# Graph attention on one core: steps summed as A (E - 1) g moved and added, and the first pass's row loads moved into the second and third cycle

## The chip, the cores and the metric

The kernel runs on one core of a Trainium2 chip. The metric is the device time of one launch in microseconds (us); lower is better.

## The reference

Two layers work on x (4096 nodes, 512 features) and a 0/1 adjacency matrix A (4096 x 4096). The first layer is attention with eight heads of 64 features each; the second is a scaled attention inside 32 blocks of 128 nodes. The change touches only the first layer:

```
feats  = einsum('nf,hfo->hno', X, W)
s_self = einsum('hno,ho->hn', feats, a_self)
s_neigh = einsum('hno,ho->hn', feats, a_neigh)
dense  = leaky_relu(s_self[:, :, None] + s_neigh[:, None, :], 0.2) * A
attn   = softmax(dense, axis=-1)
out    = relu(einsum('hij,hjo->hio', attn, feats) + b)      # then x = layernorm(x + out)
```

A pair that is no edge still has the weight exp(0) = 1. So the sum over the neighbours is the sum over all nodes plus, for the edges alone, the sum of (E - 1) feats, with E = exp(leaky_relu(...)).

## The kernel before

**Passes, chunks, steps and cycles.** The heads are worked in pairs: four passes (`r` = 0 to 3). A pass goes over four chunks (`c`) of 1024 output nodes, and a chunk over 32 steps (`j`) of 128 neighbour nodes. Steps are issued in cycles: eight steps to a cycle in passes 0 to 2 (`wide=8`: a chunk's cycles begin at j0 = 0, 8, 16, 24), four in pass 3. The "last cycle" of a chunk below is j0 = 24 in pass 0 and j0 = 28 in pass 3.

**A plain step.** VectorE makes, for each of the pair's two heads, a tile `q` of 128 x 1024 (line 1534): max(p_row, d_j) times the adjacency tile `at`. TensorE then does two things. At line 1558 it subtracts the plain features over the edges: two weight tiles `f_s` times `at`, in two halves, so four matmuls into `accf`. At line 1581 it adds `g_s` times `q` into `acc`. A mark of each `q` (ScalarE at line 1544, for one `q` in eight VectorE at line 1539) goes into `dens` (line 1597).

**A folded step**, summed as A (E - 1) g. VectorE makes `q` with two operations a head: max(p_row, d_j) times a further row `U_row` (line 1522), then minus a column `c_all`, times `at` (line 1525). The matmuls of line 1558 are left out, the matmuls of line 1581 add to `accf` and not to `acc`, and ScalarE makes both marks (line 1529). `folded(j)` says which steps are folded; it does so in passes 0 and 3 alone (`FOLDED`).

**Order within a cycle on TensorE.** Its order is the program's: the line 1558 matmuls of all the cycle's steps; transposes of adjacency for the next cycle (pass 0, line 617); in pass 3 pieces of the second layer (`PLAN`, `PLANS`); the line 1581 matmuls; after every eighth step those of line 1597; in pass 0 the sums `ae` and a second lot of transposes. The other engines' queues are filled by a planner, in the order in which it expects work to be ready; where two instructions are ready, the traces show the one that was written first going first. `in_order(True, ins)` keeps an instruction behind those written before it.

**End of a chunk.** `sums_to_rows` reads `accf` (line 1278: plus `S_col`, times `u_row`, into `ys`) and then `acc` (line 1286); `accf` and `acc` have one buffer each. Since `u_row` has one buffer too, the next chunk's is loaded after line 1278. Each of the two `p_row` has two buffers.

**Where the adjacency comes from.** In pass 0 POOL's queue loads blocks `a_b` (line 605, four bytes an element in memory, one on the chip, three buffers), TensorE transposes them, ScalarE casts them to `at` (line 628), and POOL's queue stores each to `at_d` (line 629). Later passes load `at` from `at_d` on SP's queue, which also carries `p_row` (line 1434), `u_row` (line 1440), `U_row` (line 1462), `f_s` (line 1496) and `g_s` (line 1501). In pass 0 `U_row` lies in the two buffers named `ck`.

**Buffers that the prediction uses.** The ring of `q` has 8 tiles in pass 0 and 6 in pass 3. The second layer's results in PSUM (`ps_m`) share three banks in pass 3, taken in turn.

**Second layer beside pass 3.** The pieces `a` and `b` in the plan work on two blocks of 512 nodes. In the last cycle of chunks 1 and 2 the plan says "aaba": two output products (line 1200), which VectorE reads at line 1202 into `y_f`; two value products (line 1186), read by VectorE at line 1194; the scores of the other block (line 1141), read at line 1150; two more output products.

Of the kernel before, what the change touches and what calls it, by code (L numbers as in the profile page):

```python
# [10 lines left out]
F32 = mybir.dt.float32  # L11
# [8 lines left out]
P = 128  # L20
# [378 lines left out]
def broadcast_rows(v, parts, n):  # L399

    return bass.AP(tensor=v.tensor, offset=v.offset, ap=[[0, parts], [1, n]])
# [3 lines left out]
def adjacency_streamed_path(  # L405
# [29 lines left out]
    nc = tc.nc  # L435
    N, F = x.shape
    H, _, FH = W.shape
    NT = N // P
    FC = F // P
    PR = H // 2  # L440
    FP = 2 * FH
# [3 lines left out]
    C = 1024  # L445
    CT = C // P
    NCH = N // C
# [14 lines left out]
    g_d = dram.tile([PR, NT // 4, P, 4 * FP], F32, name="g_d")  # L462
    f_d = dram.tile([PR, NT // 4, P, 4 * 2 * FP], F32, name="f_d")
    FOLDED = (0, PR - 1)
    FOLDS = {4: (1,), 5: (0, 1), 6: (0, 1, 2)}, {2: (1,), 4: (1,), 5: (0, 1), 6: (0, 1, 2)}
    HU = 2 * len(FOLDED)
    pu_d = dram.tile([2 * H + HU, N], F32, name="pu_d")
    at_d = dram.tile([NCH, NT, P, C], F32, name="at_d")
# [73 lines left out]
    rowp = ctx.enter_context(tc.tile_pool(name="rows_f", bufs=2))  # L542
    urowp = ctx.enter_context(tc.tile_pool(name="urows", bufs=1))
# [46 lines left out]
    def in_order(pinned, ins):  # L590

        if pinned:
            tc.keep_in_program_order(ins)
# [29 lines left out]
    def cast_steps(c, j, pt, steps=range(2)):  # L623

        both = pt.rearrange("p t n -> p (t n)").bitcast(FP8).rearrange("p (n k) -> p n k", k=2)
        for k in steps:
            at = ats[0, c, j + k] = ring("at", atp, 6).tile([P, C], F32R, name="at")
            ends_of_setup["ACT"] = nc.scalar.copy(at, both[:, :, k])  # L628
            nc.gpsimd.dma_start(at_d[c, j + k], at.bitcast(F32))  # L629
# [9 lines left out]
    with tc.tile_pool(name="setup1", bufs=1, side="right") as one, tc.tile_pool(  # L639
        name="setup_rows", bufs=1, side="right"  # L640
    ) as late, tc.tile_pool(name="setup2", bufs=2, side="right") as two, tc.tile_pool(
        name="xtp", bufs=4, side="right"
    ) as xtp, tc.tile_pool(name="staged1", bufs=1, side="right") as staged1, tc.tile_pool(
        name="staged2", bufs=2, side="right"
    ) as staged2, tc.tile_pool(
        name="ps_setup", bufs=3, space=PSUM
    ) as pss, tc.tile_pool(name="ps_feat", bufs=2, space=PSUM) as psf:
        NB = NT // 4
        xts, xTs, pu_js, rows = {}, {}, {}, {}
# [773 lines left out]

    steps = [(r, c, j) for r in range(PR) for c in range(NCH) for j in range(NT)]

    def main_pass(r, ae=None, wide=4):

        for c in range(NCH):
            p_row = []
            for h in range(2):  # L1430
                p_row.append(rowp.tile([P, C], F32, name=f"p_row{h}"))
                in_order(
                    r == 0 and c < 2,
                    nc.sync.dma_start(p_row[h], broadcast_rows(pu_d[2 * r + h, ts(c, C)], P, C)),
                )
            u_row = urowp.tile([P, C], F32, name="u_row")
            for h in range(2):
                in_order(
                    r == 0 and c < 2,
                    nc.sync.dma_start(  # L1440
                        u_row[h * FH : (h + 1) * FH, :],
                        broadcast_rows(pu_d[H + 2 * r + h, ts(c, C)], FH, C),
                    ),
                )
            U_row = []

            def folded(j):

                if r == PR - 1:
                    return r in FOLDED and c > 0 and j % 4 in FOLDS[c > 1].get(j // 4, ())  # L1450
                return r in FOLDED and j % 8 == 2 and (0 if c else 8) < j < NT - 8

            def rows_for_folded():

# [35 lines left out]
            for j0 in range(0, NT, wide):  # L1490
                at_step = steps.index((r, c, j0))
                cycle = range(j0, j0 + wide)
                f_s, g_s = {}, {}
                for k in range(j0 // 4, (j0 + wide) // 4):
                    f_s[k] = fsp.tile([P, 4, 2, FP], F32R, name="f_s")
                    ins = nc.sync.dma_start(
                        f_s[k].rearrange("p u s n -> p (u s n)").bitcast(F32), f_d[r, k]
                    )
                    in_order(r == 0 and c == 0 and j0 < 16, ins)
                    g_s[k] = gfp.tile([P, 4, 2, FH], F32, name="g_s")  # L1500
                    ins = nc.sync.dma_start(
                        g_s[k].rearrange("p u h o -> p (u h o)"), g_d[r, k]
                    )
                    in_order(r == 0 and c == 0 and j0 < 16, ins)
                if at_step == 0:
                    cast_steps(0, 6, last_pair)
                if any(map(folded, range(NT))) and j0 == (4 if r else 0):
                    rows_for_folded()
# [6 lines left out]
                for j in cycle:  # L1515
                    for h in range(2):
# [3 lines left out]
                        if folded(j):  # L1520
                            cn = c_all[r][:, j, h : h + 1]
                            nc.vector.scalar_tensor_tensor(
                                q, p_row[h], d_j, U_row[h], op0=OP.max, op1=OP.mult
                            )
                            nc.vector.scalar_tensor_tensor(  # L1525
                                q, q, cn, ats[r, c, j].bitcast(F32), op0=OP.subtract, op1=OP.mult
                            )
                            mark = marks[j, h] = sgp.tile([P, C], FP8, name="mark")
                            nc.scalar.activation(  # L1529
                                mark, q, AF.Sigmoid, bias=below_0, scale=2.0**80, saturate=False  # L1530
                            )
                            continue
# [5 lines left out]
                        if j % 4 == 3 and h == 1:  # L1538
                            nc.vector.tensor_scalar(  # L1539
                                mark, q, d_j, None, op0=OP.is_gt, saturate=False  # L1540
# [14 lines left out]
                for j in cycle:  # L1555
                    for w in range(0 if folded(j) else 2):
                        for s in range(2):
                            nc.tensor.matmul(  # L1558
                                accf[:, s, :],
                                f_s[j // 4][:, j % 4, w, :],  # L1560
                                ats[r, c, j][:, ts(s, HB)],
                                start=(j == 0 and w == 0),
                                stop=(j == NT - 1 and w == 1),
                            )
# [11 lines left out]
                for j in cycle:  # L1576
                    dst = accf if folded(j) else acc
                    for s in range(2):
                        for o in range(0, FP, 32):
                            h = o // FH  # L1580
# [47 lines left out]
    with tc.tile_pool(name="ps_ae", bufs=1, space=PSUM) as psx:  # L1628
        ae = psx.tile([P, HB], F32, name="ae")
        nc.vector.memset(ae, 0.0)  # L1630
        banks.append(psx)
        main_pass(0, ae, wide=8)
        banks.remove(psx)
    first_pass.close()
    banks.extend([ctx.enter_context(tc.tile_pool(name="ps_misc2", bufs=2, space=PSUM))] * 2)
    with tc.tile_pool(name="wl1", bufs=1, side="right") as wp:
        work.append(weights_of_layer_1(keep, wp))
        work.append(kind_of_graphs(wp))
        work.append(kind_of_scores(wp))
        main_pass(1, wide=8)  # L1640
        for gen in work:
            for _ in gen:
                pass
        work.clear()
    main_pass(2, wide=8)
    more.clear()
    wide_passes.close()
    with tc.tile_pool(name="lp", bufs=2) as lp, tc.tile_pool(
        name="lp1", bufs=1
# [7 lines left out]
@with_exitstack  # L1657
def tile_gat_then_graph_attention(ctx: ExitStack, tc: tile.TileContext, *args: bass.AP):
    nc = tc.nc
    keep = ctx.enter_context(tc.tile_pool(name="flag", bufs=1))  # L1660
    flag = keep.tile([1, 1], I32, name="flag")
    adjacency_streamed_path(tc, flag, *args)
    other = nc.values_load(flag[0:1, 0:1], min_val=0, max_val=1)
    with tc.If(other > 0):
        general_path(tc, *args)
# [42 lines left out]
```

## Time and profile before

| | before |
|---|---|
| three runs | 2040.04, 2040.63, 2043.24 us (median 2040.63) |
| the profiled execution | 2043.19 us |
| its span | 2041.3 us |
| TensorE matmul busy | 2005.9 us (98%) |
| VectorE busy | 1744.8 us (85%) |
| ScalarE busy | 1533.1 us (75%) |
| folded tiles of q (line 1525) | 62, for 31 steps |

The span is the profile's time from the first to the last instruction; the execution's own time has 1.9 us around it. Times in the trace count from the start of the span. A busy TensorE can hold short waits, since matmuls are pipelined and their ends are modelled; where it matters, the starts of neighbouring matmuls are compared. In a group's row the first number after the bar is busy time in us, the second the mean of one instruction in ns.

### The profile page before, as it was taken

What the parts mean: (1) busy time and instruction counts of PE and PEld (TensorE: products, weight loads), DVE (VectorE), ACT (ScalarE), POOL (GpSimd) and SP (SyncE); (2) the same over time, 40 slices, a digit from 0 to 9 for tenths busy, and PEclk for the clock granted to TensorE, in tenths of its full rate; (3) what the DMA queues carried; (4) which work ended last, traced back from release to release, by engine and by line L of the source; (5) the groups of instructions that cost most, each with busy time, mean ns of one, the idle gap of its engine ahead of it and who ended that gap; (6) DMA issues with size and microseconds to landing.
All of it is one profiled execution on the core that took longest, in us unless ns stands there. A gap on an engine that the chain in (4) does not pass through costs nothing.

```text
span 2041.3 us, 38200 instructions
## 1 busy us (share of the span) xinstructions
PE 2005.9 (98%) x14981; PEld 1030.0 (50%) x14981; DVE 1744.8 (85%) x2219; ACT 1533.1 (75%) x1872; POOL 231.0 (11%) x362
## 2 busy tenths in 40 slices
PE   8999999999999999999999999999999999999997
PEld 7885545444444444444444544444444444445443
DVE  5668898898999998798999989999997897889754
ACT  3348988788888889788899889999786566567420
POOL 1222222222200000000000000000020210211111
PEclk9999999999999999999999999999999999999999
DMA  6899999999999999788999999989975775775211
GB/s 206 240 320 280 283 286 288 285 280 282 316 377 342 346 359 342 261 311 292 318 321 338 313 328 338 335 277 368 323 277 186 249 255 173 232 273 176 73 55 44
DMA packets 209386, 558.70 MB, mean 274 GB/s; under 512 B 25052, under 2 KB 66012, under 8 KB 209196
## 3 DMA queue, kind: packets, MB, share of 16 engines
q1 hardware_dynamic: 144844, 433.65, 61.0%
q0 software_dynamic: 62272, 121.98, 23.3%
q8 instruction: 120, 1.97, 0.4%
q10 hardware_dynamic: 2080, 0.52, 0.1%
q14 instruction: 70, 0.57, 0.1%
HBM read 499.13 MB, written 107.28 MB: 297 GB/s over the span
## 4 chain that ended last, share of the span: by engine, by line
PE 85%; DMA 7%; DVE 5%; issue 1%; ACT 1%; SPq 0%; POOL 0%; POOLq 0%; DVEq 0%; ACTq 0%
PE acc L1581 35%; PE accf L1558 20%; PE ps_fe L818 5%; PE ps_m L1186 5%; PE ps_m L1114 5%; PE dens L1597 5%; DMA a_b<-in_adj_dram 4%; DVE q L1534 3%; PE accf L1581 2%; PE ps_m L1141 1%; PE ps_m L1200 1%; DMA hp_l<-hs_d 1%; PE ps_m L617 1%; DMA at_d<-at 1%; PE ps_m L1043 1%
## 5 line engine op out<-in xcount | busy, mean ns | idle before, releaser
L1534 DVE SCALAR_TENSOR_TENSOR q<-p_row,d_all,at 128x1024 f32<-128x1024 f32 x962 | 1168.1, 1279 | 106.0 <-PE acc L1581 78.8
L1544 ACT ACTIVATE mark<-q,nb_all 128x1024 fp8e4<-128x1024 f32 x834 | 926.8, 1144 | 174.7 <-DVE q L1534 160.1
L1581 PE MATMUL acc<-q,g_s 128*32 128x512 f32 x7696 | 853.7, 594 | 1.1 <-DVE q L1534 0.4
L1581 PEld LDWEIGHTS acc<-q,g_s 128*32 128x32 f32 x7696 | 250.2, 110 | 557.2 <-issue 496.3
L1558 PE MATMUL accf<-at,f_s 128*128 128x512 f32 x1924 | 469.3, 400 | 1.7 <-ACT at L628 1.6
L1558 PEld LDWEIGHTS accf<-at,f_s 128*128 128x128 f32 x1924 | 357.2, 189 | 107.3 <-issue 27.8
L1249 ACT ACTIVATE ck<-ck,neg_half_f 128x1024 f32<-128x1024 f32 x128 | 146.0, 1141 | 28.5 <-DMA ck<-in_adj_dram 28.4
L1250 ACT ACTIVATE ck<-ck,neg_quarter 128x1024 f32<-128x1024 f32 x128 | 146.3, 1143 | 1.8
L1597 PE MATMUL dens<-mark,e_b 128*6 128x512 fp8e4 x2048 | 125.3, 379 | 2.5 <-DVE mark L1539 2.5
L818 PE MATMUL ps_fe<-w_sb_f,xT_f 128*128 128x264 f32 (+1 forms) x512 | 121.6, 395 | 1.7 <-ACT xT_f L730 1.7
L628 ACT CAST at<-ps_m 128x1024 fp32r<-128x1024 fp8e4 x124 | 116.3, 1022 | 4.8 <-issue 2.0
L1186 PE MATMUL ps_m<-wvT,x1T 128*128 128x512 f32 x256 | 114.2, 594 | 0.0
L1114 PE MATMUL ps_m<-x1T,M_sb 128*128 128x512 f32 x256 | 113.1, 595 | 0.0
L818 PEld LDWEIGHTS ps_fe<-w_sb_f,xT_f 128*128 128x128 f32 x512 | 100.5, 200 | 16.2 <-ACT xT_f L730 2.3
L1372 POOL DMA_DIRECT2D hs_d<-hst x12 | 10.7, 896 | 828.1 <-DVE hst L1362 817.5
L1539 DVE TENSOR_SCALAR mark<-q,d_all 128x1024 fp8e4<-128x1024 f32 x128 | 96.2, 751 | 4.7
L629 POOL DMA_DIRECT2D at_d<-at x128 | 69.1, 540 | 272.5 <-ACT at L628 94.0
L1597 PEld LDWEIGHTS <-e_b 128*6 128x6 bf16 x2048 | 55.9, 86 | 80.1 <-issue 38.2
L1529 ACT ACTIVATE mark<-q,below 128x1024 fp8e4<-128x1024 f32 x62 | 69.6, 1153 | 24.5 <-DVE q L1525 24.2
L1114 PEld LDWEIGHTS ps_m<-x1T,M_sb 128*128 128x128 f32 x256 | 48.0, 190 | 58.9 <-issue 57.1
L1525 DVE SCALAR_TENSOR_TENSOR q<-q,c_all,at 128x1024 f32<-128x1024 f32 x62 | 77.3, 1273 | 0.0
L1186 PEld LDWEIGHTS ps_m<-wvT,x1T 128*128 128x128 f32 x256 | 47.7, 190 | 56.3 <-issue 55.1
(207 smaller groups left out, 1294.9 us busy)
## 6 DMA issues: line engine op xcount, KB each, us to landing
at<-at_d SPq DMA_DIRECT2D x384, 512.0 KB, 6.1
f_s<-f_d SPq DMA_DIRECT2D x128, 512.0 KB, 7.8
at_d<-at POOLq DMA_DIRECT2D x128, 512.0 KB, 19.1
ck<-in_adj_dram SPq DMA_DIRECT2D x128, 512.0 KB, 5.5
g_s<-g_d SPq DMA_DIRECT2D x128, 256.0 KB, 5.9
f_d<-fst POOLq DMA_DIRECT2D x16, 1024.0 KB, 7.5
a_b<-in_adj_dram POOLq DMA_DIRECT2D x32, 512.0 KB, 21.7
p_row<-pu_d SPq DMA_DIRECT2D x32, 512.0 KB, 6.7
```

The lines of the kernel that those rows point to most:

```text
L628: ends_of_setup["ACT"] = nc.scalar.copy(at, both[:, :, k])
L818: nc.tensor.matmul(pf[:, q, :, cols], tile_j(xTs[k][:, c].rearrange("p u n -> p (u n)"), u), w_sb[:, c, 4 * q : 4 * q + 4, cols], start=(c ...
L1114: nc.tensor.matmul(pz, L1["M"][:, f, ts(c, P)], x1T[:, f, :], start=(f == 0), stop=(f == FC - 1),)
L1186: nc.tensor.matmul(pv, x1T[:, f, ts(u, P)], L1["wvT"][:, f, :], start=(f == 0), stop=(f == FC - 1),)
L1249: tc.keep_in_program_order(nc.scalar.activation(ck, ck, AF.Square, bias=neg_half))
L1250: nc.scalar.activation(ck, ck, AF.Abs, bias=neg_quarter, accum_out=binp[:, k : k + 1])
L1534: ends_of_setup["Q"] = nc.vector.scalar_tensor_tensor(q, p_row[h], d_j, ats[r, c, j].bitcast(F32), op0=OP.max, op1=OP.mult)
L1539: nc.vector.tensor_scalar(mark, q, d_j, None, op0=OP.is_gt, saturate=False)
L1544: nc.scalar.activation(mark, q, AF.Sigmoid, bias=nb_all[:, j, hh : hh + 1], scale=BIG, saturate=False,)
L1558: nc.tensor.matmul(accf[:, s, :], f_s[j // 4][:, j % 4, w, :], ats[r, c, j][:, ts(s, HB)], start=(j == 0 and w == 0), stop=(j == NT - 1 an ...
L1581: nc.tensor.matmul(dst[o : o + 32, s, :], g_s[j // 4][:, j % 4, h, o % FH : o % FH + 32], qs[j, h][:, ts(s, HB)], start=(j == 0), stop=(j ...
L1597: nc.tensor.matmul(dens[lo : lo + 6, :], e_b[:, j, 2 * r + h, :], marks[j, h][:, ts(s, HB)], start=(j == 0), stop=(j == NT - 1),)
```

## The change

Which steps are folded: in pass 0 they were j = 10 and 18 in chunk 0 and j = 2, 10, 18 in chunks 1 to 3 (11 in all); now they are j = 8, 16, 24 in every chunk (12). In pass 3 they were six in chunk 1 and seven each in chunks 2 and 3 (20); now chunks 1 and 2 have j = 28 and 29 as well (24). Of a block of `f_s` that has folded steps, only the stretch from its first to its last plain step is loaded. In pass 0 `u_row` of chunks 1 to 3 is asked for in the chunk's second cycle, and both `p_row` of the next chunk in the third cycle, all kept in program order.

```diff
-    FOLDS = {4: (1,), 5: (0, 1), 6: (0, 1, 2)}, {2: (1,), 4: (1,), 5: (0, 1), 6: (0, 1, 2)}
+    FOLDS = {1: {4: (1,), 5: (0, 1), 6: (0, 1, 2), 7: (0, 1)}, 2: {2: (1,), 4: (1,), 5: (0, 1), 6: (0, 1, 2), 7: (0, 1)}, 3: {2: (1,), 4: (1,), 5: (0, 1), 6: (0, 1, 2)}}
...
+    p_rows = {}
+
+    def load_p_rows(r, c, pinned):
+
+        rows = []
+        for h in range(2):
+            rows.append(rowp.tile([P, C], F32, name=f"p_row{h}"))
+            ins = nc.sync.dma_start(rows[h], broadcast_rows(pu_d[2 * r + h, ts(c, C)], P, C))
+            in_order(pinned, ins)
+        return rows
+
+    def load_u_row(r, c, pinned):
+
+        u_row = urowp.tile([P, C], F32, name="u_row")
+        for h in range(2):
+            ins = nc.sync.dma_start(
+                u_row[h * FH : (h + 1) * FH, :],
+                broadcast_rows(pu_d[H + 2 * r + h, ts(c, C)], FH, C),
+            )
+            in_order(pinned, ins)
+        return u_row
...
         for c in range(NCH):
-            p_row = []
-            for h in range(2):
-                p_row.append(rowp.tile([P, C], F32, name=f"p_row{h}"))
-                in_order(
-                    r == 0 and c < 2,
-                    nc.sync.dma_start(p_row[h], broadcast_rows(pu_d[2 * r + h, ts(c, C)], P, C)),
-                )
-            u_row = urowp.tile([P, C], F32, name="u_row")
...
+            p_row = p_rows.pop((r, c), None) or load_p_rows(r, c, (r, c) == (0, 0))
+            if r or c == 0:
+                u_row = load_u_row(r, c, r == 0)
...
-                    return r in FOLDED and c > 0 and j % 4 in FOLDS[c > 1].get(j // 4, ())
-                return r in FOLDED and j % 8 == 2 and (0 if c else 8) < j < NT - 8
+                    return r in FOLDED and c > 0 and j % 4 in FOLDS[c].get(j // 4, ())
+                return r in FOLDED and j % 8 == 0 and j > 0
...
+                    live = [u for u in range(4) if not folded(4 * k + u)]
                     ins = nc.sync.dma_start(
-                        f_s[k].rearrange("p u s n -> p (u s n)").bitcast(F32), f_d[r, k]
+                        f_s[k][:, live[0] : live[-1] + 1].rearrange("p u s n -> p (u s n)").bitcast(F32),
+                        f_d[r, k, :, live[0] * 2 * FP : (live[-1] + 1) * 2 * FP],
                     )
...
+                if r == 0 and c and j0 == 8:
+                    u_row = load_u_row(r, c, True)
+                if r == 0 and c < NCH - 1 and j0 == 16:
+                    p_rows[r, c + 1] = load_p_rows(r, c + 1, True)
```

More of the change, by code (lines that the diff above doesn't have):

```diff
@@ L1424, in adjacency_streamed_path @@
     steps = [(r, c, j) for r in range(PR) for c in range(NCH) for j in range(NT)]
+    p_rows = {}
[15 more added lines that the diff above has]
+        return u_row
     def main_pass(r, ae=None, wide=4):
         for c in range(NCH):
-            p_row = []
-            for h in range(2):
-                p_row.append(rowp.tile([P, C], F32, name=f"p_row{h}"))
-                in_order(
-                    r == 0 and c < 2,
-                    nc.sync.dma_start(p_row[h], broadcast_rows(pu_d[2 * r + h, ts(c, C)], P, C)),
-                )
-            u_row = urowp.tile([P, C], F32, name="u_row")
[L1437 to L1444, printed above, removed]
+            p_row = p_rows.pop((r, c), None) or load_p_rows(r, c, (r, c) == (0, 0))
+            if r or c == 0:
+                u_row = load_u_row(r, c, r == 0)
             U_row = []
```

## The prediction

> **What bounds the kernel now.** I read the busy shares first, then the rows of the operations concerned, then pass 0 and pass 3 cycle by cycle, since an average over the span hides where a wait ends last. From the page:
>
> ```profile
> PE 2005.9 (98%) x14981; PEld 1030.0 (50%) x14981; DVE 1744.8 (85%) x2219; ACT 1533.1 (75%) x1872; POOL 231.0 (11%) x362
> L1525 DVE SCALAR_TENSOR_TENSOR q<-q,c_all,at 128x1024 f32<-128x1024 f32 x62 | 77.3, 1273 | 0.0
> L1558 PE MATMUL accf<-at,f_s 128*128 128x512 f32 x1924 | 469.3, 400 | 1.7 <-ACT at L628 1.6
> ```
>
> TensorE has only 35 us without a matmul in flight, so a matmul removed is time gained wherever VectorE keeps up. Line 1558 costs 469.3/1924 = 0.244 us each; a fold removes four, 0.98 us, and adds two VectorE operations of 77.3/62 = 1.25 us.
>
> Busy time by stretch, last cycle of pass 0's chunk 1 and first two of chunk 2 (columns: span, PE, PEld, DVE, ACT, POOL, granted clock, DMA share, GB/s):
>
> ```profile
> 343.00:369.00 26.00, 26.00 (x248) 13.33 (x246) 22.18 (x21) 23.15 (x23) 5.73 (x10) 1.00 1.10 303
> 369.00:401.00 32.00, 28.00 (x245) 12.49 (x243) 25.47 (x30) 24.75 (x26) 7.70 (x13) 0.95 1.12 258
> 401.00:427.00 26.00, 26.00 (x248) 13.07 (x246) 24.35 (x25) 22.83 (x23) 6.08 (x10) 1.00 1.12 283
> ```
>
> A chunk's first cycle takes 32 us where its neighbours take 26, and DMA is full throughout. The waits of TensorE in pass 0, its timeline and that of SP say why:
>
> ```profile
> PE ps_m L617 <- DMA a_b<-in_adj_dram: 6.2, 3, 3.6
> ...
> 379.89 1.07 PE L617 MATMUL ps_m<-ident_b,a_b 128*128 128x128 bf16 x16 [3.63 <-DMA a_b<-in_adj_dram]
> ...
> 352.38 1.09 SPq L1440 DMA_DIRECT2D u_row<-pu_d  x2
> ...
> 362.38 1.51 SPq L1434 DMA_DIRECT2D p_row<-pu_d  x2
> ...
> 352.91 26.93 DMA a_b<-in_adj_dram
> ```
>
> The three waits (0.41, 3.63 and 2.19 us) stand in the first cycles of chunks 1, 2 and 3. Each late block was asked for at a chunk's end, beside 0.5 MB of `u_row` and 1 MB of `p_row`, and took 26.5 to 28 us; the median is 21.7. After the 3.63 us TensorE ran slowly too: line 1581's weight loads stand 0.86 us apart for 3.4 us, against 0.43, another 1.7 us. Recoverable: 6.2 + 1.7 = 7.9 us.
>
> Pass 3, last cycle of chunk 1 (chunk 2's is alike), timelines of VectorE and TensorE:
>
> ```profile
> 1568.74 3.68 DVE L1534 SCALAR_TENSOR_TENSOR q<-p_row,d_all,at 128x1024 f32<-128x1024 f32 x3 [8.14 <-PE accf L1581]
> 1573.00 6.06 DVE L1534 SCALAR_TENSOR_TENSOR q<-p_row,d_all,at 128x1024 f32<-128x1024 f32 x5
> 1578.98 0.74 DVE L1202 SCALAR_TENSOR_TENSOR y_f<-ps_m,rd_f,x1b 128x512 f32<-128x512 f32 x1
> 1579.64 1.27 DVE L1278 SCALAR_TENSOR_TENSOR ys<-accf,S_col,u_row 128x1024 f32<-128x1024 f32 x1
> ...
> 1577.53 1.88 PE L1200 MATMUL ps_m<-v_t,a 128*128 128x512 f32 x4
> 1579.24 7.03 PE L1186 MATMUL ps_m<-wvT,x1T 128*128 128x512 f32 x16
> ...
> 1610.96 3.11 PE L1581 MATMUL acc<-q,g_s 128*32 128x512 f32 x16 [0.21 <-DVE q L1534]
> ```
>
> VectorE idles 8.14 us, but before these q tiles, since the ring of six is full; it then works without a gap until it reads the first output product at 1578.98. Half a chunk on, TensorE already waits for q.
>
> [...] after the 3.63 us gap 3.4 us at half speed, none after the 2.19 us one. [...] SP's rows beside POOL's `a_b`, DMA share 1.10. [...]
>
> **The change part by part.**
>
> *Pass 0, matmuls.* Three folds leave first cycles, four enter last ones, those of third cycles stay: 12 for 11, net -0.98 us.
>
> *Pass 0, VectorE in the last cycle.* It has 3.7 us idle around line 1278 (2.16 + 1.54 in chunk 1); the fold's second operations take 2.4 at the 1.2 us pitch. Line 1278 now needs the fold's g too, 1.75 us into the line 1581 phase. By then step 28's q is ready to start and was written first, so I take line 1278 to follow step 31's q: `accf` is then read about 5 us before the next chunk's first matmul. Zero. Were it put ahead, step 31's q would be 0.5 us late in each of four chunks: 0 to +2.
>
> *Pass 0, rows.* `u_row` (0.5 MB) moves from near 352 to 288 in chunk 1's example, `p_row` (1 MB) from 362 to 314, behind `g_s` on SP; neither buffer is then in use and both rows are wanted over 40 us later. `U_row` (1 MB, in `ck`) is released by step 24, not 18, so its load moves towards the border, from 318 to about 342. Near the late block 1.5 MB leave and 1 MB comes 10 us ahead of it; `f_s` is 128 KB smaller in three blocks a chunk. At 290 GB/s, 0.6 MB less is 2 us of traffic, and it starts earlier. The block has some 23.5 us from request to use; one asked for at 340.37 landed after 22.8. So I take the two smaller waits and the clock loss as gone and 1 us of the large one as left: -7. Both ends: 0 (the waits only move) and -7.9.
>
> *Pass 3, matmuls.* Four folds: 4 x 0.98 = -3.9 us, in two last cycles.
>
> *Pass 3, VectorE ahead of the PSUM reads.* From 1568.74 VectorE makes eight q and a mark; now four of these need a second operation, 4 x 1.2 = 4.8 us, so line 1202's first read moves from 1578.98 to 1583.8 and ends at 1584.4. Who waits: the second value product takes the first output product's bank, three banks in turn. It would begin 1.95 us earlier than now (f is shorter), at 1580.8, so TensorE waits 3.6 us. Net in each of chunks 1 and 2: -1.95 + 3.65 = +1.7. If the planner put the reads between the q it would be -1.95; but reads that came late in cycle 20 (line 1150, ready near 1536, done from 1540.8) stood behind q there.
>
> *Pass 3, line 1278.* It leaves 1579.64, where nobody waited, for 3.5 us into the line 1581 phase, 1.2 us in a stretch where VectorE ends 0.2 us late already; some 0.9 us of idling before the `y_f` scaling takes most of it: +0.4 a chunk, 0 to +1.2. Ahead of step 31's q it would cost 2 us.
>
> *Clock.* A 3.6 us gap may or may not halve the clock: 0 to +1.7 each. I take half for one of two, +0.8.
>
> *Marks, casts, smaller `f_s` in pass 3.* The number of marks and their engine stay (no fold has j % 4 = 3); ScalarE idles 10.65 us in the pass 3 cycle; the transfers saved there (2.4 MB) end well ahead of need. Zero; DMA share is 0.73 there, so a loss is excluded.
>
> **Sum:** -0.98 - 7 + 2 x 1.7 + 2 x 0.4 + 0.8 = -3.0 us: span 2038.3 from 2041.3. That execution took 2043.19 us, above the median of 2040.63 by what runs differ; taken off the median: 2037.6.
>
> **The rivals.**
>
> *Faster: the planner reads PSUM in time.* Pass 3 then gives -3.9 + 0.8 and pass 0 -8.9: -12 at best, -10 with 2 us left: 2029 to 2031. For it: one read moved ahead of two q suffices. Against: the order in cycle 20.
>
> *Slower: the border waits stay.* DMA share is over 1 in every cycle of pass 0, so `a_b` may be late for lack of bandwidth, with `U_row` taking the rows' place. It decides where a block asked for at the border lands more than 26 us later. Pass 0 is then -1, pass 3 +4.2 to +7.6 with both clock losses: 2044 to 2047. Against: only the three blocks beside the rows were late.
>
> *It does not do what it says.* If the planner issued the pinned rows no earlier than before, or pass 3 swallowed its folds (0), pass 0 alone decides: 2032 to 2040.
>
> **How the numbers follow.** 0.2% is 4.1 us, about what a measurement of this kernel can tell from no change. Main case 0.45, centre -3.0, from -6 to +1, a bit under a third of it beyond -4.1. Faster rival 0.27, nearly all beyond. Slower rival 0.16, nearly all beyond +4.1. Last case 0.12, half beyond -4.1. Faster 0.13 + 0.26 + 0.06 = 0.45, which I raise to 0.48 for the lower bound of the PSUM wait; slower 0.16; same 0.36. The main case alone: 2034.6 to 2041.6. With the faster rival's middle and the slower rival's low half: 2029.5 to 2046.
>
> **What would show it.** Line 1558 x1904, line 1525 x72. Waits of line 617 for `a_b` under 2 us in pass 0, and first cycles of chunks 2 and 3 near 27 us. `p_row` in mid-chunk and `U_row` near a chunk's end on SP. In pass 3's last cycles of chunks 1 and 2 a gap of 3 to 4 us between the two value products, with line 1202 as releaser: absent, the faster rival is right. `a_b` landing later than 26 us with waits as large as before: the slower one is. Line 1278 ahead of step 31's q would add to either.

## The result, and the profile after

| | before | changed kernel |
|---|---|---|
| median of 22 runs each | 2040.05 us | 2043.58 us |
| the profiled execution | 2043.19 us | 2043.83 us |
| its span | 2041.3 us | 2042.0 us |

The changed kernel takes 1.0014 of the time before, 95% interval [1.0007, 1.0020]: 2.9 us slower, where 3.0 us faster was forecast. (The medians lie 3.5 us apart; the ratio, which has the interval, is used below.) The time lies inside the range given, on the wrong side of no change, and by less than the 0.2% that was called the limit of telling. (The two profiled spans differ by less than the medians: the profile of before was a long execution.)

The page of the changed kernel, busy shares and rows (the first number after the bar is busy time in us, the second the mean of one in ns, then idle time ahead of it):

```profile
PE 2007.2 (98%) x14961; PEld 1025.5 (50%) x14961; DVE 1754.9 (86%) x2229; ACT 1525.8 (75%) x1872; POOL 224.7 (11%) x362
L1573 PE MATMUL accf<-at,f_s 128*128 128x512 f32 x1904 | 464.8, 399 | 3.0 <-ACT at L628 2.2
L1186 PE MATMUL ps_m<-wvT,x1T 128*128 128x512 f32 x256 | 120.5, 619 | 7.8 <-DVE y_f L1202 7.1
L1540 DVE SCALAR_TENSOR_TENSOR q<-q,c_all,at 128x1024 f32<-128x1024 f32 x72 | 90.7, 1276 | 0.0
```

The plain matmuls (line 1558 before, 1573 now) went from 1924 to 1904 and the folded tiles (line 1525 before, 1540 now) from 62 to 72, as the diff says. TensorE is nonetheless 1.3 us longer busy: the value products of line 1186 now wait 7.1 us for `y_f`, and one of them takes 619 ns on average. Of the waits of TensorE, these two answer to what was forecast:

```profile
PE ps_m L1186 <- DVE y_f L1202: 7.1, 2, 3.6
...
PE ps_m L617 <- DMA a_b<-in_adj_dram: 0.2, 1, 0.2
```

The waits for the adjacency blocks in pass 0 went from 6.2 us to 0.2. In their place stand two waits of 3.6 us for line 1202, in pass 3. In the timeline of TensorE, last cycle of pass 3's chunk 1 (start, duration, work, and in brackets the idle time ahead of it with its releaser):

```profile
1566.37 1.88 PE L1200 MATMUL ps_m<-v_t,a 128*128 128x512 f32 x4
1568.08 3.60 PE L1186 MATMUL ps_m<-wvT,x1T 128*128 128x512 f32 x8
1575.25 6.60 PE L1186 MATMUL ps_m<-wvT,x1T 128*128 128x512 f32 x8 [3.57 <-DVE y_f L1202]
1581.69 3.73 PE L1141 MATMUL ps_m<-x1T,zT 128*128 128x128 f32 x32
```

The second value product waits 3.57 us, and the same eight matmuls then take 6.60 us instead of 3.60: half clock. The trace records half speed for 6.8 us from 1574.3 on, while TensorE still waits, and as long at the gap in chunk 2, where the eight matmuls take 6.37 us. With the clock full they take 3.70 us after such a gap (a second trace, below), so these two gaps cost 3.57 us of waiting each, and 2.9 and 2.7 us more. The reason stands on VectorE, same place:

```profile
1573.26 1.28 DVE L1549 SCALAR_TENSOR_TENSOR q<-p_row,d_all,at 128x1024 f32<-128x1024 f32 x1
1574.45 1.40 DVE L1202 SCALAR_TENSOR_TENSOR y_f<-ps_m,rd_f,x1b 128x512 f32<-128x512 f32 x2
```

The PSUM read follows the last `q` of step 31, though the products it reads had been done since 1568. Busy time by stretch (span, PE, PEld, DVE, ACT, POOL, granted clock, DMA share, GB/s), last cycle of pass 0's chunk 1 and first two of chunk 2:

```profile
340.10:365.50 25.40, 25.19 (x237) 12.13 (x237) 23.12 (x21) 23.37 (x24) 7.40 (x11) 1.00 1.11 300
365.50:392.50 27.00, 26.65 (x245) 13.34 (x244) 24.15 (x29) 22.47 (x23) 6.10 (x10) 1.00 1.12 281
392.50:418.10 25.60, 25.60 (x241) 12.63 (x241) 23.94 (x25) 22.02 (x23) 6.32 (x10) 1.00 1.11 287
```

The first cycle of chunk 2 takes 27.0 us where it took 32.0. DMA share is as high as before, 1.11 and 1.12.

From the two traces, cycle by cycle: pass 0 is 7.9 us shorter; the last cycles of pass 3's chunks 1 and 2 are 4.9 and 4.7 us longer (the cycles after them give and take up to 1.6 us each, nothing in sum); pass 1 is 1.3 us longer. That sums to about the measured 2.9 us, but by luck: the two spans differ by 0.7 us only, since this execution reached pass 0 3.2 us sooner (157.0 us against 160.2; 158.5 in its second trace), and the stretches at half clock change from one execution to the next. Whether such a pair of traces speaks for all executions is what the experiments had to say.

### The profile page after: what moved, and what is told of

Read it like the earlier page. It is cut to its first block, busy times and chain, and to the rows that moved or that the text cites. A ratio compares the mean times of both kernels' runs of the same rounds, so it can differ in the third digit from the quotient of the medians.

```text
span 2042.0 us, 38108 instructions
## 1 busy us (share of the span) xinstructions
PE 2007.2 (98%) x14961; PEld 1025.5 (50%) x14961; DVE 1754.9 (86%) x2229; ACT 1525.8 (75%) x1872; POOL 224.7 (11%) x362
## 5 line engine op out<-in xcount | busy, mean ns | idle before, releaser
L1549 DVE SCALAR_TENSOR_TENSOR q<-p_row,d_all,at 128x1024 f32<-128x1024 f32 x952 | 1155.0, 1279 | 108.7 <-PE acc L1596 58.6
L1559 ACT ACTIVATE mark<-q,nb_all 128x1024 fp8e4<-128x1024 f32 x824 | 906.7, 1148 | 145.1 <-DVE q L1549 134.4
L1596 PE MATMUL acc<-q,g_s 128*32 128x512 f32 x7616 | 842.0, 593 | 1.0
L1573 PEld LDWEIGHTS accf<-at,f_s 128*128 128x128 f32 x1904 | 351.5, 189 | 110.0 <-issue 26.5
L1544 ACT ACTIVATE mark<-q,below 128x1024 fp8e4<-128x1024 f32 x72 | 81.8, 1146 | 84.6 <-DVE q L1540 84.1
L1186 PE MATMUL ps_m<-wvT,x1T 128*128 128x512 f32 x256 | 120.5, 619 | 7.8 <-DVE y_f L1202 7.1
L1540 DVE SCALAR_TENSOR_TENSOR q<-q,c_all,at 128x1024 f32<-128x1024 f32 x72 | 90.7, 1276 | 0.0
```

The source lines that it names most:

```text
L1186: nc.tensor.matmul(pv, x1T[:, f, ts(u, P)], L1["wvT"][:, f, :], start=(f == 0), stop=(f == FC - 1),)
L1549: ends_of_setup["Q"] = nc.vector.scalar_tensor_tensor(q, p_row[h], d_j, ats[r, c, j].bitcast(F32), op0=OP.max, op1=OP.mult)
L1559: nc.scalar.activation(mark, q, AF.Sigmoid, bias=nb_all[:, j, hh : hh + 1], scale=BIG, saturate=False,)
L1573: nc.tensor.matmul(accf[:, s, :], f_s[j // 4][:, j % 4, w, :], ats[r, c, j][:, ts(s, HB)], start=(j == 0 and w == 0), stop=(j == NT - 1 an ...
L1596: nc.tensor.matmul(dst[o : o + 32, s, :], g_s[j // 4][:, j % 4, h, o % FH : o % FH + 32], qs[j, h][:, ts(s, HB)], start=(j == 0), stop=(j ...
```

## The experiments

Theory: pass 0 gains, and the two waits in pass 3, with the clock, take back more. Below, "lost to the clock" means (1 - granted clock) times the span, averaged over a kernel's runs; in the traces of before and of the changed kernel the granted clock is either 1.00 or 0.50. It counts half speed in which TensorE waits as well. "Before" was run again on the chip of each set: 2038.61, 2038.78 and 2038.63 us.

**The two passes apart.** The first-pass part alone: the changed kernel without the folds of steps 28 and 29.

```diff
-    FOLDS = {1: {4: (1,), 5: (0, 1), 6: (0, 1, 2), 7: (0, 1)}, 2: {2: (1,), 4: (1,), 5: (0, 1), 6: (0, 1, 2), 7: (0, 1)}, 3: {2: (1,), 4: (1,), 5: (0, 1), 6: (0, 1, 2)}}
+    FOLDS = {1: {4: (1,), 5: (0, 1), 6: (0, 1, 2)}, 2: {2: (1,), 4: (1,), 5: (0, 1), 6: (0, 1, 2)}, 3: {2: (1,), 4: (1,), 5: (0, 1), 6: (0, 1, 2)}}
```

> The changed kernel without the folds of steps 28 and 29 in chunks 1 and 2 of pass 3. Theory (the last pass loses what the first gains): the time falls by about 9.4 us against the changed kernel, to about 7.5 us under the kernel before (ratio to it 0.9963), with no wait of line 1186 for line 1202 and no half-speed clock in pass 3. Rival (the first pass gains nothing in most executions, its gain is the luck of one profile): the time stays within 2 us of the kernel before.

The last-pass part alone: the kernel before with the changed `FOLDS` and

```diff
-                    return r in FOLDED and c > 0 and j % 4 in FOLDS[c > 1].get(j // 4, ())
+                    return r in FOLDED and c > 0 and j % 4 in FOLDS[c].get(j // 4, ())
```

> The kernel before with nothing but the folds of steps 28 and 29 in chunks 1 and 2 of pass 3. Theory: about 9.4 us slower than before (ratio 1.0046): in each of the two chunks TensorE waits some 3.6 us for the PSUM read and then runs 6.8 us at half clock. Rival (the cost comes only together with the first pass's changes, or the two cycles alone pay 1.7 us each as in the prediction): 0 to 4 us slower.

The first pass alone: 2034.94 us, ratio 0.9982 [0.9976, 0.9989], a gain of 3.7 us. The last pass alone: 2046.43 us, 1.0041 [1.0027, 1.0055], a loss of 8.4 us. The row of the value products in the first-pass kernel:

```profile
L1186 PE MATMUL ps_m<-wvT,x1T 128*128 128x512 f32 x256 | 114.3, 594 | 0.0
```

The same row in the last-pass kernel:

```profile
L1186 PE MATMUL ps_m<-wvT,x1T 128*128 128x512 f32 x256 | 119.3, 614 | 7.8 <-DVE y_f L1202 7.2
```

The wait belongs to the folds of steps 28 and 29 wholly. Of the last-pass kernel's loss, 8.15 us between the means, 4.0 us is lost to the clock (15.2 +- 1.2 us against 11.2 +- 0.3; each +- here is one standard error) and 4.15 us is at full clock. The first pass gave half of what the traces had promised.

**Rows or places of the folds.** The changed kernel with the rows asked for at a chunk's start again, and then, second diff, the changed rows with the folds of before (pass 3's too, as in the first-pass kernel).

```diff
-            p_row = p_rows.pop((r, c), None) or load_p_rows(r, c, (r, c) == (0, 0))
-            if r or c == 0:
-                u_row = load_u_row(r, c, r == 0)
+            p_row = p_rows.pop((r, c), None) or load_p_rows(r, c, r == 0 and c < 2)
+            u_row = load_u_row(r, c, r == 0 and c < 2)
...
-                if r == 0 and c and j0 == 8:
-                    u_row = load_u_row(r, c, True)
-                if r == 0 and c < NCH - 1 and j0 == 16:
-                    p_rows[r, c + 1] = load_p_rows(r, c + 1, True)
```

> The changed kernel with p_row and u_row of pass 0 asked for at the chunk's start as before, folds as changed. Theory (the rows' traffic at the border makes the adjacency blocks late): the waits of line 617 come back, 4 to 8 us slower than the changed kernel, so 7 to 11 us slower than before. Rival (no folds in the first cycle is what freed it): within 1.5 us of the changed kernel.

```diff
-                return r in FOLDED and j % 8 == 0 and j > 0
+                return r in FOLDED and j % 8 == 2 and (0 if c else 8) < j < NT - 8
```

> The kernel before with the rows of pass 0 asked for in the second and third cycles, folds as before in both passes. Theory (the rows alone do it): the waits of line 617 for the adjacency are gone, 6 to 8 us faster than before (ratio 0.9962 to 0.997). Rival (the folds' places do it): within 2 us of before.

Rows at the start: 2043.57 us, 1.0028 [1.0019, 1.0036]. Rows alone: 2038.13 us, 1.0003 [0.9995, 1.0011]. TensorE's wait for adjacency in the kernel with the rows at the start:

```profile
PE ps_m L617 <- DMA a_b<-in_adj_dram: 0.8, 2, 0.6
```

The same wait in the kernel with the rows alone:

```profile
PE ps_m L617 <- DMA a_b<-in_adj_dram: 3.4, 1, 3.4
```

Moving the rows back does not bring the waits back: 0.8 us. Moving the rows alone takes chunk 2's wait away and makes chunk 3's larger. TensorE's timeline there:

```profile
480.91 1.89 PE L617 MATMUL ps_m<-ident_b,a_b 128*128 128x128 bf16 x16 [3.44 <-DMA a_b<-in_adj_dram]
```

After it the trace has 6.8 us at half clock. That block was asked for at 458.15, in POOL's timeline, and landed 22.8 us later:

```profile
458.15 0.90 POOL L605 DMA_DIRECT2D a_b<-in_adj_dram  x1 [1.51 <-DMA at_d<-at]
```

The same request in the changed kernel:

```profile
454.54 0.90 POOL L605 DMA_DIRECT2D a_b<-in_adj_dram  x1 [1.40 <-DMA at_d<-at]
```

Since the kernels do not begin chunk 3 at the same time, count from the first matmul of line 1558 or 1573 in the chunk. Before asked for this block 17 us ahead and it took 26.3 to 27.1 us; the rows alone 12.3 us ahead, 22.8 us; the rows at the start with the new folds 17.8 us ahead, 26.0 us; the changed kernel 14.8 us ahead (18.1 in its second trace), 22.5 us. So the rows' traffic does go with a longer transfer, as the prediction had it, but with the rows alone POOL asked some 5 us later, and the wait stayed. The total hides this too: against before, the rows alone are 2.0 +- 0.5 us faster at full clock and lose 1.8 +- 0.6 us more to the clock (13.0 against 11.2). And at this one border rows still pass: pass 1's first `p_row`, 1 MB, in SP's timeline of the kernel with the rows alone:

```profile
463.60 1.52 SPq L1433 DMA_DIRECT2D p_row<-pu_d  x2
```

With the new folds and the moved rows all three waits are gone. The new folds bring smaller `f_s` loads with them, since steps 8, 16 and 24 stand first in their blocks (384 KB and not 512, nine times before chunk 3; by estimate 4 us of traffic at this stretch's 284 GB/s). All kernels with the full blocks waited 3.4 us or more, all with the smaller ones 0.8 us or less, and no run separates the two. Against 1.0028 with the rows at the start, the changed kernel has 1.0014 and 1.0015 in two sets, with intervals that just overlap: beside the new folds, the rows' place is worth some 2.8 us by these ratios.

**How fast the waits of before vary.** The kernel before, profiled twice more.

> The kernel before once more, for its trace. Theory (the adjacency waits of pass 0 differ from one execution to the next, and the profiled execution of before, 2043.19 us beside a median of 2040, was a bad one): waits of line 617 for a_b under 5 us in sum, and not the same chunks' waits as large. Rival (they are a fixed cost of this kernel): 6.2 us again, 3.6 in chunk 2.

> The kernel before a third time, for its trace. As b1: theory, waits of line 617 for a_b that differ by several us from the first trace's 6.2; rival, 6.2 again.

TensorE's wait for adjacency in the first of these:

```profile
PE ps_m L617 <- DMA a_b<-in_adj_dram: 5.2, 2, 3.0
```

And in the second:

```profile
PE ps_m L617 <- DMA a_b<-in_adj_dram: 5.3, 2, 2.8
```

The first cycle of chunk 2, also in the second, in the view of stretches:

```profile
369.10:398.10 29.00, 25.86 (x237) 11.99 (x234) 24.95 (x28) 23.91 (x25) 7.43 (x12) 1.00 1.12 263
```

The waits are nearly fixed: 6.2, 5.2 and 5.3 us in three executions, and 6.2 in the last-pass kernel, whose pass 0 is that of before. The half clock after the largest is not: the first trace had it (granted clock 0.95, 32.0 us), the next two did not (1.00, 29.0 us here), and the last-pass kernel had 3.4 us of it after one of two waits of 3.1 us. So this term of the forecast was seen in two traces of four.

**The changed kernel again, and three ways past the wait.** These four ran in one set. First the changed kernel as it is.

> The changed kernel once more, beside the next three on one chip. Theory: 3 to 5 us slower than before (the first pass's -3.3 us and the last pass's +8.1 us of the single changes, summed), with a granted clock about 0.0015 to 0.002 lower than the same kernel without the last pass's folds. Rival (the two parts don't add): within 1.5 us of before.

It took 2041.35 us, 1.0015 [1.0006, 1.0023]. In this trace the same two gaps were followed by a single 3.4 us of half clock, where the first trace had 6.8 us twice. The gap in chunk 2 was followed by none:

```profile
1745.38 3.70 PE L1186 MATMUL ps_m<-wvT,x1T 128*128 128x512 f32 x8 [3.57 <-DVE y_f L1202]
```

That cycle, at full clock, takes 28.48 us from its first matmul to the next cycle's, where before takes 26.48.

Where a gap falls goes with it. In the trace of before the clock was half for 3.41 us from 380.88 on, in the first trace of the changed kernel for 6.83 us from 1574.30 on and again from 1744.96, with 163.8 us at full clock between, 48 times 3.41. Divide those two traces from 170 us to the end of pass 3 into windows of 3.41 us on these times: TensorE was idle for 71% (before), 77% and 63% (changed) of the three windows after which the clock fell, and for at most 42% of any other. (Ahead of that time, with other matmuls, it fell after a window idle for 34% too, in the changed kernel at 154.35.) Three windows of this trace, in the view of stretches:

```profile
1573.09:1576.50 3.41, 1.05 (x3) 0.58 (x4) 3.41 (x5) 2.93 (x3) 0.00 (x0) 1.00 0.92 317
1740.35:1743.76 3.41, 1.46 (x4) 0.38 (x2) 3.41 (x4) 0.97 (x2) 0.00 (x0) 1.00 0.96 327
1743.76:1747.17 3.41, 1.79 (x4) 0.87 (x5) 3.41 (x6) 2.97 (x3) 0.00 (x0) 1.00 0.93 296
```

The first gap leaves TensorE 1.05 us of work in one window (idle for 69%), and the next is at half clock. The second gap, as long, lies across two windows with 1.46 and 1.79 us of work (idle for 57% and 48%), and the clock stays full. A second 3.41 us at half clock followed where the gap still took 28% and 42% of the first (changed kernel, first trace), and not where it took nothing of it (before). This is read from the traces; no run moved a gap to test it.

Next, one folded step in place of two:

```diff
-    FOLDS = {1: {4: (1,), 5: (0, 1), 6: (0, 1, 2), 7: (0, 1)}, 2: {2: (1,), 4: (1,), 5: (0, 1), 6: (0, 1, 2), 7: (0, 1)}, 3: {2: (1,), 4: (1,), 5: (0, 1), 6: (0, 1, 2)}}
+    FOLDS = {1: {4: (1,), 5: (0, 1), 6: (0, 1, 2), 7: (0,)}, 2: {2: (1,), 4: (1,), 5: (0, 1), 6: (0, 1, 2), 7: (0,)}, 3: {2: (1,), 4: (1,), 5: (0, 1), 6: (0, 1, 2)}}
```

> The changed kernel with step 28 folded and step 29 plain in chunks 1 and 2 of pass 3. VectorE's chain ahead of line 1202 is two operations (2.4 us) shorter and TensorE arrives 0.98 us later, so the wait of line 1186 falls from 3.6 us to about 0.2. Theory [...]: no half-speed stretch, 6 to 9 us faster than the changed kernel, more than the 2 x 3.4 - 2 x 0.98 = 4.9 us of the waits alone. Rival (the cost goes with the number of folds): half of it, 3 to 5 us faster.

2033.49 us, 0.9974 [0.9966, 0.9983]: 5.3 us faster than before and 7.9 us faster than the changed kernel, the best of all kernels here. TensorE's timeline at the same place:

```profile
1574.90 3.70 PE L1186 MATMUL ps_m<-wvT,x1T 128*128 128x512 f32 x8 [0.27 <-DVE y_f L1202]
```

Two second operations fewer ahead of the read, about 2.4 us, and one f stretch 0.98 us longer: 3.57 - 3.4 is 0.2, and 0.27 is what is left. The clock stays full there. Next, both folds kept, but the `q` of steps 30 and 31 written after the pieces of the second layer, so that the planner may put the PSUM reads ahead of them (`make_q` is the loop that makes `q` and marks):

```diff
+                late = r == PR - 1 and c in (1, 2) and j0 == NT - wide
+                make_q(cycle[:2] if late else cycle)
...
                 if r:
                     pieces(c, j0 // 4, 0)
+                if late:
+                    make_q(cycle[2:])
```

> The changed kernel, both folds kept, but the q of steps 30 and 31 of those two cycles are written behind the pieces of the second layer, so VectorE takes line 1202's first read two operations (2.4 us) earlier. Theory: the wait falls from 3.6 to about 1.2 us[...]; 7 to 11 us faster than the changed kernel. Rival (VectorE's extra 4.8 us of work in each cycle is what costs): the time lost moves to the q of step 30 or 31, less than 4 us faster.

2036.00 us, 0.9989 [0.9982, 0.9996], 5.4 us faster than the changed kernel. VectorE's timeline of this kernel:

```profile
1572.10 1.28 DVE L1540 SCALAR_TENSOR_TENSOR q<-p_row,d_all,U_row 128x1024 f32<-128x1024 f32 x1
1573.30 0.75 DVE L1202 SCALAR_TENSOR_TENSOR y_f<-ps_m,rd_f,x1b 128x512 f32<-128x512 f32 x1
```

And TensorE's, where its second line is from the end of the same cycle:

```profile
1570.54 7.25 PE L1186 MATMUL ps_m<-wvT,x1T 128*128 128x512 f32 x16
...
1589.60 1.48 PE L1604 MATMUL acc<-q,g_s 128*32 128x512 f32 x10 [0.38 <-DVE q L1552]
```

The read now lies between `q` operations and the two value products run as one block: with the same work to do, the order on VectorE sets the wait. But 7 to 11 us had been expected. The cycle takes 26.53 us, as long as before (26.50) and not 2 us less: the `q` of steps 30 and 31 now come late, and from line 1604's first matmul there to the next cycle it takes 10.4 us where it took 8.7. Last, the wait left in length but filled with work: four matmuls of a zero block, added to the first value product.

```diff
+            for f in range(FC if u == 2 and blk in (0, 2) else 0):
+                nc.tensor.matmul(
+                    pv[:64],
+                    ident[:64, 64:],
+                    L1["wvT"][:64, f, :],
+                    start=False,
+                    stop=(f == FC - 1),
+                    skip_group_check=True,
+                )
```

> The changed kernel with four matmuls of a block of zeros (3.5 us) added onto the first value product in the two cycles, so that TensorE works while it waits for line 1202; the sum stays what it was. The wait is as long as before, but TensorE is not idle. Theory (half of the last pass's cost is the clock): no half-speed stretch there, 4 to 6 us faster than the changed kernel. Rival (the clock falls for another reason, or costs little): the same time, or up to 1 us slower.

2037.29 us, 0.9995 [0.9986, 1.0003]; TensorE's timeline there (the zero matmuls, which the trace counts as eight, stand under line 1194):

```profile
1570.39 3.60 PE L1186 MATMUL ps_m<-wvT,x1T 128*128 128x512 f32 x8
1573.91 3.64 PE L1194 MATMUL ps_m<-wvT,ident_f 64*64 64x512 f32 x8
1577.54 3.70 PE L1186 MATMUL ps_m<-wvT,x1T 128*128 128x512 f32 x8
```

The second value product begins as late as with the wait (7.15 us after the first, 7.17 in the changed kernel), yet it takes 3.70 us and the kernel is 4.1 us faster than with the empty gap. No half clock is left in pass 3. Lost to the clock: 10.2 +- 0.5 us against 14.1 +- 0.7 in the changed kernel, while the rest of the time is alike (2027.6 and 2027.3 us). So of the two waits' cost some 4 us is the clock alone; both cycles take 28.48 us, as at full clock above.

**The casts in pass 0.** One fold in pass 3, as in the best kernel, and pass 0's folds in the third step of a cycle and not the first.

```diff
-                return r in FOLDED and j % 8 == 0 and j > 0
+                return r in FOLDED and j % 8 == 2 and j > 8
```

> The kernel of e5 (one fold in each of the last pass's two cycles) with the first pass's folds at j = 10, 18, 26 in every chunk in place of 8, 16, 24. The folded step is then the third of its cycle, so ScalarE's marks for it stand behind the casts of the next steps. Theory: the 0.4 to 0.5 us that line 1558's matmuls wait for a cast in each last cycle are gone; line 1278, behind step 31's q anyway, does not mind; 1 to 2 us faster than e5, so 6 to 7.5 us faster than before. Rival (the casts are late for the fold's work on VectorE, wherever it stands, or line 1278 now holds something up): within 1 us of e5 or slower.

2039.30 us, 0.9999 [0.9991, 1.0007], where 6 to 7.5 us faster than before had been expected. Pass 0's last cycles got 0.89 to 0.96 us shorter than before, and not some 0.43 as in the changed kernel: the cast that stands behind the folded step's mark on ScalarE was the missing half microsecond. But the wait for adjacency came back in chunk 3, in TensorE's timeline

```profile
483.50 1.89 PE L617 MATMUL ps_m<-ident_b,a_b 128*128 128x128 bf16 x16 [4.74 <-DMA a_b<-in_adj_dram]
```

with 3.4 us of half clock after it, and the gain was lost. Here, as with the rows alone, POOL's queue asked for the block late, 12.8 us ahead of the chunk, and 18.2 in the kernel with one fold, which differs from this one only in pass 0's folds. What makes the request some 5 us later was not settled: step 10 stands third in its block, so the `f_s` loads are full again too.

## Why the prediction was wrong, point by point

**Pass 3, the wait: right.** Order on VectorE, waiting product, releaser and length were as worked out (3.57 us against 3.6). Net of the clock, the last-pass kernel lost 4.15 us where 2 x 1.7 + 2 x 0.4 = 4.2 was taken, and where the clock stayed full the last cycle was 2.0 us longer than before, in one trace of the changed kernel and twice in that with the wait filled. The totals are less close: against the first-pass kernel the changed one lost only 2 to 3 us at full clock. Of line 1278's 0.4 a chunk nothing can be seen by itself, since the cycles after the border sum to nothing.

**Pass 3, the clock: mis-sized.** The term was +0.8, half of one of two by the author's estimate, with 1.7 us each as its end: 3.4 us at half speed, as after the 3.63 us gap in the trace of before. The last-pass kernel lost 4.0 us to the clock, and filling the gaps gave back about as much. A single gap was followed by 0, 3.4 or 6.8 us at half clock, and cost up to 2.9 us so. After the same two gaps of 3.57 us it was 6.8 and 6.8 us in one execution of the changed kernel, 3.4 us and none in another. With three of these four followed by half clock, a gap of 3.6 us should have been priced as likely to trip, with 6.8 us at half speed as the end.

**Pass 0, the rows and the folds: the larger error.** The term was -7 for the rows, and -8.0 with the matmuls; the first pass alone measured -3.7. The step that failed is the size: one trace of before was taken for what every execution has to give back, and a fold for 0.98 us wherever it stands. What the runs put in place of its parts: the waits are 5.7 us as a mean of four traces, not 6.2, and all go; the clock's 1.7 us stood in two of the four, and over the runs 1.0 us less is lost to the clock in the first-pass kernel (10.2 us against 11.2). Folds in the last cycles gained some 0.42 us and not 0.98, four times, since the cast was costed at zero: ScalarE's idle time in a whole cycle was looked at, and not what stands behind the mark in its queue. First cycles lost 0.57 us and not 0.98 by becoming plain, three times (27.01 us against 26.44 where neither waits). So the folds gave nothing in pass 0, where -0.98 was taken. ScalarE's timeline in the changed kernel, last cycle of pass 0's chunk 1:

```profile
339.69 1.15 ACT L1544 ACTIVATE mark<-q,below 128x1024 fp8e4<-128x1024 f32 x1 [2.38 <-DVE q L1540]
342.00 3.74 ACT L628 CAST at<-ps_m 128x1024 fp32r<-128x1024 fp8e4 x4
```

TensorE's timeline there:

```profile
343.05 3.95 PE L1573 MATMUL accf<-at,f_s 128*128 128x512 f32 x16 [0.21 <-ACT at L628]
```

The mark waits for the folded `q`, the casts stand behind the marks, the matmuls wait for the cast. Pass 1 is 0.5 us longer in the first-pass kernel's trace. So -5.7 - 1.0 + 0.5 = -6.2, which agrees with the traces (a span of 2033.7 us against 2039.7 as the mean of three of before) and not with the measured interval (-4.9 to -2.2 us about -3.7). The executions traced were not typical: those of before lay 3.1, 3.2 and 1.1 us above the medians of their sets, that of the first-pass kernel 0.6. That is 1.9 of the 2.5 us. Which of the waits are shorter in the other executions no trace shows.

**Pass 0, the mechanism: half right.** The waits went, as forecast, and first cycles came near 27 us. With the rows moved, transfers at the border of chunk 3 were shorter (22.5 to 25.1 us, three kernels) than with the rows there (26.0 to 27.1). But the prediction kept the time of the request, "some 23.5 us from request to use"; with the rows alone the block had 19.3 us, and the total did not change (1.0003). The time at which POOL asks moves with the folds' places, or with the smaller `f_s` loads that come with them: this cause stays open.

**The sum.** For the first pass -3.7 in place of -8.0; for the last pass, as the changed kernel less the first-pass kernel (1.0014 less 0.9982), +6.5 in place of +5.0. Of the 5.9 us between forecast and result 4.3 are thus pass 0's and the rest pass 3's. The last pass measured by itself gave +8.4 (5.5 to 11.2), so the two parts add up within their intervals. The slower rival ended on the right side for the wrong reason: its border waits did not stay, while its "both clock losses" did. Line 1278 stands after step 31's `q`, and `p_row` and `U_row` on SP lie where they were expected.

## What to carry to other kernels

Before work is put on an engine, look at which reads of PSUM stand behind it in its queue and which matmul wants their bank: here VectorE had 8.14 us idle ahead of these `q` in the trace of before, and TensorE still waited 3.57 us for the read behind them. A TensorE gap of 3.57 us cost up to 2.9 us more through the clock, in some executions, so price one like it with 6.8 us at half speed, or shrink it (one fold in place of two was the best version) or fill it. The 2.19 us gap in the trace of before was followed by no half clock; by the windows above, one under some 1.9 us would not trip it, an estimate (0.57 x 3.41 us). A loss that one trace shows, above all one of the clock, is worth a second trace before it is counted as gain, and the traced execution is worth comparing with the median.

## What was not expected of the hardware

- **A gap costs twice over, and not always.** The same 3.57 us gap was followed by 6.8 us, 3.4 us or none at half clock; gaps of 3.44 and 4.74 us by 6.8 and 3.4 us; one of 3.63 us by 3.4 us, and of two of 3.1 us in one execution one by 3.4 us and one by none. In the windows of 3.41 us above, from the traces of before and of the changed kernel, what tells them apart is how long TensorE is idle in one: the clock fell after those idle for 63% to 77%, and not after those idle for up to 57%.
- **Zero matmuls were worth their time.** 3.64 us of them in each gap made the kernel 4.1 us faster than leaving the gap empty, with every later instruction at the same place in the order.
- **A late block need not be a slow one.** The block that stalled TensorE for 3.44 us landed 22.8 us after its issue, faster than the 26.9 us of the one that stalled it before, in chunk 2; it was asked for 12.3 us ahead of its chunk, and that one 16.3.
